# A third matmul level in one more round, stores moved to another queue, and a new table for side work

## The chip, the cores and the metric

The kernel runs on one core of a Trainium2 chip. The metric is the time of one execution on the device in microseconds (us); the median of several runs stands for a kernel. One execution was also profiled. Engines go by these names: PE (TensorE, matmuls), PEld (its weight loads), DVE (VectorE), ACT (ScalarE), POOL (GpSimd), and SP (SyncE, which here only issues DMAs). ACT and POOL issue DMAs too. Each engine works through its own queue in order.

## The reference

Two blocks, each with a residual, on x of shape (32, 128, 2048), in float32:

```python
x = x + L0_ffn(L0_cond(x, cond_128, ...), W, bias, A, Bf, coeffs, scales)
x = x + L1_ffn(L1_cond(x, cond_128, weight, c_weight, fside), up, down, perm)

# L0_cond: a mix of 8 kernels of 128x128 for each of 32 items
att = softmax(mlp(cond));  agg_w = einsum('bk,koi->boi', att, weight)
out = einsum('boi,bih->boh', agg_w, x) + (att @ bias_k)[:, :, None]
# L0_ffn: a dense 2048x2048 product with 16 low-rank updates
out = einsum('bsd,od->bso', x, W) + bias + updates(A, Bf, coeffs * scales)
# L1_cond: grouped convolution over the 2048 columns, 9 taps
# L1_ffn: a permutation of the columns, 16 heads of 128 -> 512 -> 128 with gelu, permuted back
```

The change concerns the dense product of L0_ffn (its weight, with the updates added in, is called W below) and the making of the mixed kernels agg_w.

## The kernel before

**The dense product.** It is done by a scheme that replaces eight products of half-size blocks by seven, nested. The outer seven are the *rounds* P1, P2, P6, P7, P5, P3, P4 in this order (`ROUNDS`). Each round goes over eight groups of four items, so a *step* is one round and one group, and the steps 0 to 7 of a round come one after the other. Inside a step the same seven-product scheme is used again (`multiply`): 28 matmuls of 512 columns. Two further functions take two neighbouring steps together, a *pair* (an even step, then an odd one):

- `multiply_third` (L579): the inner products P2 and P4 of both steps are not done one by one but by a third level, as seven *quarter* products (L603, matmuls of 256 columns at L611) that are all done in the odd step. The five other inner products stay (L598). A pair has 40 matmuls of 512 columns and 28 of 256.
- `multiply_more` (L484): the inner products P3 and P7 too are done at the third level. There are now two families of quarters (0 for P2 and P4, 1 for P3 and P7), three inner products (P1, P5, P6; matmuls at L501), and 24 matmuls of 512 columns and 56 of 256 (L516) in a pair. The even step does the quarters P1 and P2 of both families, the odd step the rest.

`PAIRS` says which pairs of a round have a third level, `MORE` which have it for P3 and P7 too: one pair of P6, three of P7, three of P3.

**Accumulators.** Each product sits in one of eight PSUM banks and is added by DVE to accumulators in SBUF (L497, L591), a quarter at L529 or L619. A quarter of family 1 needs a second addition of 256 columns (L534). Products that share a bank follow each other: quarters P1, P6, P7 and P4 of a family, and P5 and P3. Rounds P1 to P3 add to one accumulator, P5 to two (`ADDED`: u1 to u3 and u2 to c11). The accumulators come from DRAM (`part_load`) and go back (`part_store`) at the end of the odd step. P1 starts them: its first sums are copied by ACT (L593).

**Inputs and weights.** POOL makes the sums that the scheme needs: of x at L283 and L319 to L322 for a step ahead, of two steps at L444 (`third_inputs`) and L472 to L475 (`more_inputs`), of the weights at L252 to L256 (`inner_weights`), L401 to L407 (`third_weights`) and L462 (`more_weights`, whose second half DVE does at L1319). All of this lives in 26 equal SBUF buffers; a load waits for the last reader of the tile that had its buffer.

**W itself** is made in round P1: `w_make` for the first four blocks, `w_make_two` (L218) for twelve more, two ahead of each of steps 0 to 5, on PE (L223) and DVE (L226). The blocks are stored to DRAM (`w_store`, L168) through POOL's queue.

**Mixed kernels.** `mixed_kernel` (L708) makes an item's mixed 128x128 kernel by eight DVE operations (L716 the first, L718 the others). There are 256 of these. They are laid in between the products of a step, at the places `between(0)` to `between(3)` (a *turn* below): two at each in most steps of P2, P6, P7, P5 and P3, one in some, and 16 in all in the last two steps of P1. Each finished kernel is stored through ACT (L720).

Of the kernel before, what the change touches and what calls it, by code (L numbers as in the profile page):

```python
# [17 lines left out]
B = 32  # L18
L = 2048
QW = 512  # L20
KEXP = 8
# [11 lines left out]
NG = B // GB  # L33
# [18 lines left out]
    "P1": (0, 1, 2, 3), "P2": (0, 1, 2, 3), "P6": (0, 1, 2, 3), "P7": (0, 1, 2, 3),  # L52
    "P5": (0, 1, 2, 3), "P3": (0, 1, 2, 3), "P4": (0,),
}
MORE = {"P6": (1,), "P7": (1, 2, 3), "P3": (1, 2, 3)}
ENDS = ("P1", "P4")
EARLY = 2

# [2 lines left out]
def adaln_ffn_kernel(  # L61
# [16 lines left out]
    nc = tc.nc  # L78
# [85 lines left out]
        nc.sync.dma_start(t.rearrange("p k o c -> p (k o c)"), WT[kh, oh, kc])  # L164
        return t

    def w_store(k, t):
        nc.gpsimd.dma_start(wb_d[k], t.rearrange("p k o c -> p (k o c)"))  # L168

    def w_make(k, t, between=lambda: None):  # L170

# [46 lines left out]
    def w_make_two(ks, ts, sa, tb):  # L218
        pxs, pys, pzs = ([bank() for _ in ks] for _ in range(3))

        def product(n, ps, first, last, ki, oi):
            for (_, _, kc), p, t in zip(ks, ps, ts):
                nc.tensor.matmul(  # L223
                    p, lhsT=sa[n][:, kc], rhs=tb[n], start=first, stop=last, skip_group_check=True
                )
                nc.vector.tensor_tensor(t[:, ki, oi], p, t[:, ki, oi], ALU.add)  # L226

        product("P1", pxs, True, False, 0, 0)
        product("P2", pzs, True, True, 0, 0)
        done(*pzs)  # L230
        product("P6", pxs, False, False, 0, 1)
        product("P5", pys, True, False, 1, 1)
        product("P7", pxs, False, False, 1, 1)
        product("P3", pys, False, True, 0, 1)
        done(*pys)
        product("P4", pxs, False, True, 1, 0)
        done(*pxs)
        for k, t in zip(ks, ts):
            w_store(k, t)

    def row_sums(oh, t):
        for ki in range(2):
# [33 lines left out]
    def part_store(n, g, t, eng=nc.gpsimd):  # L276
        eng.dma_start(part_d[n, g], t.rearrange("p k s c -> p (k s c)"))
# [301 lines left out]
    def multiply_third(r, g, lhs, rhs, olds, between, quarters, sq):  # L579

        px, py = bank(), bank()
        accs = olds if olds[0] is not None else [slot(f"m_{r}{g}", (P, 2, 2, QW))]
        fresh = set()
        if sq:
            both = [held.pop(), accs]

        def add(si, oi, ps):
            for acc in accs:
                to = acc[:, si, oi]
                if olds[0] is not None or (si, oi) in fresh:  # L590
                    nc.vector.tensor_tensor(to, ps, to, ALU.add)  # L591
                else:
                    nc.scalar.copy(to, ps)  # L593
            fresh.add((si, oi))

        def product(k, ps, first, last):
            for kc in range(4):
                nc.tensor.matmul(  # L598
                    ps, lhsT=lhs[k][:, bass.ts(kc, P)], rhs=rhs[k][kc],
                    start=first and kc == 0, stop=last and kc == 3, skip_group_check=True,  # L600
                )

        def quarter(k, to):  # L603

            if k in ("P1", "P5", "P2"):
                qs[k] = bank()
            ps = qs[{"P6": "P1", "P7": "P1", "P4": "P1", "P3": "P5"}.get(k, k)]
            first, last = k in ("P1", "P2", "P5"), k in ("P2", "P3", "P4")
            for i, out in enumerate(halves(ps)):
                for kc in range(2):  # L610
                    nc.tensor.matmul(  # L611
                        out, lhsT=sq[k][:, i, bass.ts(kc, P)], rhs=quarters[i][k][kc],
                        start=first and i == 0 and kc == 0, stop=last and i == 1 and kc == 1,
                        skip_group_check=True,
                    )
            b, h = to
            for acc in both[b]:
                part = acc[:, :, 0, h * NQ : (h + 1) * NQ]
                nc.vector.tensor_tensor(  # L619
                    part, ps.rearrange("p (s n) -> p s n", s=2), part, ALU.add  # L620
                )
            if last:
                done(ps)

        qs = {}
        turns = [
            (("P1", (0, 0)), ("P2", (0, 0))), (("P6", (0, 1)), ("P5", (1, 1))),
            (("P7", (1, 1)), ("P3", (0, 1))), (("P4", (1, 0)),),
        ]

        def turn(n, now):
            if sq and now:
                for k, to in turns[n]:
                    quarter(k, to)

        early = r not in ENDS
        product("P1", px, True, False)
        add(0, 0, px)
        between(0)
        turn(0, early)  # L640
        if sq:
            sums_rest(nc.vector)
        product("P5", py, True, False)
        add(1, 1, py)
        between(1)
        turn(1, early)
        product("P6", px, False, False)
        add(0, 1, px)
        between(2)
        turn(2, early)  # L650
        product("P3", py, False, True)
        add(0, 1, py)
        done(py)
        between(3)
        turn(3, early)
        product("P7", px, False, True)
        add(1, 1, px)
        add(1, 0, px)
        done(px)
        turn(0, not early)  # L660
        between(4)
        turn(1, not early)
        turn(2, not early)
        between(5)
        turn(3, not early)
        if not sq:
            held.append(accs)
            return
        for b, accs in enumerate(both):
            for (_, new), acc in zip(ADDED[r], accs):  # L670
                part_store(new, g - 1 + b, acc, nc.sync)

    held = []

# [542 lines left out]
    olds = {}  # L1217
    chain = small()
    nxt, waiting, ts, quarter_ops, more_ops = {}, {}, {}, [], []
    heads = [(g, h) for g in range(NG) for h in range(NH)]  # L1220

    def olds_load(i):
# [3 lines left out]
    for i, (r, g) in enumerate(steps):  # L1226
        ri = i // NG
        last_round = ri + 1 == len(ROUNDS)
        if g == 0:
            b = (ri - 1) * (NG - 2) + 2  # L1230
            mixes = [(b + n // KEXP, n % KEXP) for n in range((NG - 2) * KEXP)]
            mixes = [m for m in mixes if m[0] < B]
        if i + 1 < len(steps):
            if i + 1 not in xs:
                xs[i + 1] = x_loads(*steps[i + 1])
# [62 lines left out]
        def between(j):  # L1298

            if j == 3 and 0 <= k_early < EARLY:  # L1300
                outer_sums(k_early, early_x)

            b = (ri - 1) * (NG - 2) + g + 1 if ri > 0 else g - (NG - 2)
            if (g in range(1, NG - 1) if ri > 0 else g >= NG - 2) and b < B and r not in MORE:
                k = j - 2 if r == "P5" and g == 1 else j
                if 0 <= k < KEXP // 2:
                    mixed_kernel(b, (2 * k, 2 * k + 1))
            if r in MORE and 0 < g and j < 4:
                for _ in range(1 if g in (2, 4) else 2):
                    if mixes:  # L1310
                        b, k = mixes.pop(0)
                        mixed_kernel(b, (k,))
            if ri == 0 and j == 2:
                for k in blocks[6 + 2 * g : 8 + 2 * g]:
                    wt[k] = w_load(*k)
            if i and j < 4 and quarter_ops:
                nc.vector.tensor_tensor(*quarter_ops.pop(0), ALU.subtract)
            if j < 4 and more_ops:
                nc.vector.tensor_tensor(*more_ops.pop(0), ALU.subtract)  # L1319
            if i == NG - 1 and j == 3:  # L1320
                olds_load(i + 1)
            if j == 3 and ahead and steps[i + 2][0] == "P6":
                xs[i + 2] = x_loads(*steps[i + 2])
            if ri == 0 and unsummed and (j in (1, 3) and (i, j) != (1, 3) or (i, j) == (3, 2)):
                row_sums(*unsummed.pop())
            if (i, j) in ((2, 5), (3, 0), (3, 4), (4, 0)) and unsummed_first:
                t = unsummed_first.pop(0)
                tt = nc.vector.tensor_tensor
                tt(wsum[:, 0, 0], wsum[:, 0, 0], t[:, 0, 0], ALU.add)
                tt(wsum[:, 0], wsum[:, 0], t[:, 1], ALU.add)  # L1330
            if last_round:
                if j == 1 and i + 1 < len(steps):
                    lhs[i + 1] = x_combine(*steps[i + 1], xs.pop(i + 1))
                    olds_load(i + 1)
                if j == 4 and i + 2 < len(steps):
                    xs[i + 2] = x_loads(*steps[i + 2])
                if j in (2, 4):
                    stage(k0 + j // 2, stage_first)
                if j % 2:
                    stage_third(k0 + j // 2)  # L1340
                else:
                    stage(k0 + j // 2, stage_second)
# [25 lines left out]
        if g == NG - 1 and ri + 1 < len(ROUNDS):  # L1368
            rhs = nxt
            nxt = {}  # L1370

    before = None
    for k, (g, h) in enumerate(heads):
# [83 lines left out]
```

## Time and profile before

| | |
|---|---|
| time, median of 3 runs | 2572.88 us (2571.82 to 2573.05) |
| the profiled execution | 2571.83 us, its span 2570.1 us |
| granted PE clock | 0.999 |
| PE busy | 2557.3 us |
| DVE busy | 1622.3 us |
| POOL busy | 1425.2 us |
| ACT busy | 532.4 us |
| round P5, pairs 0 to 3 (first product to first product) | 46.4 us each |
| round P3, pairs 1 to 3 | 45.0, 45.7, 45.1 us |

A window of the trace gives each engine's busy time in a pair. P5's pairs 1 to 3 are the windows from 895.1, 941.5 and 987.9 us, P3's those from 1080.8, 1125.8 and 1171.5. In them DVE is busy for 35.5, 35.6 and 26.7 us in P5 (the last has no mixed operations), and 33.6, 29.4 and 34.4 us in P3; POOL for 22.5, 25.4 and 25.9 us in P5, and 44.3, 37.6 and 38.9 us in P3. Lines of the page and of the trace name an engine, a line of the kernel, the operation, the tiles written and read, and shapes; what stands after an arrow is who ended the wait. In a timeline the first two numbers are the start and the length in us of operations that were merged (x2, x3).

### The profile page before, as it was taken

Reading aid. Unit: us, or ns where it says so; the run is one execution under the profiler, and the core shown is the slowest. Engines: PE = TensorE matmul, PEld = TensorE weight load, DVE = VectorE, ACT = ScalarE, POOL = GpSimd, SP = SyncE. Lnnn points to the kernel's source line nnn. Section 1 sums busy time; section 2 is a strip of 40 time slices with the busy share of each in tenths; the row PEclk is TensorE's granted clock in tenths of the full one; section 3 lists DMA queues with packets and bytes.
Section 4 is the critical chain, followed back from the end, with each engine's and each line's share of the span. In section 5 each row is a group of like instructions: output and inputs, shape, how many; then the busy total and the mean of one; then the engine's idle time right before and its main releaser. Section 6 shows DMA issues by size and latency. Waiting matters only on the chain.

```text
span 2570.1 us, 22392 instructions
## 1 busy us (share of the span) xinstructions
PE 2557.3 (100%) x7238; PEld 1373.2 (53%) x7238; DVE 1622.3 (63%) x2505; ACT 532.4 (21%) x1099; POOL 1425.2 (55%) x1182
## 2 busy tenths in 40 slices
PE   9999999999999999999999999999999999999998
PEld 4555555565566555566554454455554555555543
DVE  5575576676767777667477666666666666666610
ACT  0000000000000000000011344444434444444432
POOL 8532788889997846988532144444334434434222
PEclk9999999999999999999999999999999999999999
DMA  7552588569366586674866987777776787777432
GB/s 294 209 214 117 197 342 345 207 266 394 148 247 265 207 344 261 232 286 163 280 235 206 296 292 253 222 250 239 227 224 228 249 254 221 221 248 241 165 120 90
DMA packets 186868, 610.44 MB, mean 238 GB/s; under 512 B 17664, under 2 KB 91904, under 8 KB 142336
## 3 DMA queue, kind: packets, MB, share of 16 engines
q1 hardware_dynamic: 147936, 473.48, 51.4%
q0 software_dynamic: 32992, 132.14, 15.3%
q10 hardware_dynamic: 5824, 3.40, 0.5%
q8 instruction: 58, 0.95, 0.1%
q14 instruction: 58, 0.48, 0.1%
HBM read 372.45 MB, written 202.94 MB: 224 GB/s over the span
## 4 chain that ended last, share of the span: by engine, by line
PE 98%; DVE 2%; DMA 0%; issue 0%; POOLq 0%; ACT 0%; ACTq 0%; DVEq 0%
PE bank L598 24%; PE bank L990 17%; PE bank L1001 17%; PE bank L611 8%; PE bank L846 6%; PE bank L516 6%; PE bank L501 6%; PE bank L357 5%; PE bank L754 4%; PE bank L223 3%; PE bank L180 1%; DVE ags L718 1%; DMA w<-in_WT 0%; PE bank L157 0%; DVE u L497 0%; DVE u L529 0%
## 5 line engine op out<-in xcount | busy, mean ns | idle before, releaser
L990 PE MATMUL bank<-t,ws 128*128 128x512 f32 x1024 | 460.3, 592 | 0.0
L1001 PE MATMUL bank<-gl,ws 128*128 128x512 f32 x1024 | 460.2, 592 | 0.0
L1008 POOL DMA_INDIRECT out<-t,orow x128 | 153.1, 1196 | 547.6 <-DVE t L1006 471.6
L993 ACT ACTIVATE gl<-bank 128x512 f32<-128x512 f32 x512 | 306.2, 598 | 433.4 <-PE bank L990 424.0
L1001 PEld LDWEIGHTS bank<-gl,ws 128*128 128x128 f32 x1024 | 194.6, 190 | 233.0 <-issue 231.3
L990 PEld LDWEIGHTS bank<-t,ws 128*128 128x128 f32 x1024 | 194.6, 190 | 226.6 <-issue 223.1
L1006 DVE TENSOR_TENSOR t<-bank,t 128x512 f32<-128x512 f32 x128 | 88.5, 691 | 324.0 <-PE bank L1001 322.8
L739 POOL TENSOR_TENSOR x<-x,fb 128x512 f32<-128x512 f32 x128 | 174.7, 1393 | 178.3 <-DMA x<-in_x 139.2
L745 ACT ACTIVATE bank<-w,aggb 128x512 f32<-128x512 f32 x128 | 80.8, 684 | 876.7 <-DMA w<-w_d 864.2
L598 PE MATMUL bank<-P_t,s_P 128*128 128x512 f32 x576 | 255.6, 592 | 0.4 <-ACT m_P L593 0.4
L283 POOL TENSOR_TENSOR xt<-xt,xt 128x512 f32<-128x512 f32 x120 | 158.0, 1348 | 88.8 <-DMA xt<-in_xT 70.5
L718 DVE SCALAR_TENSOR_TENSOR ags<-mix,att_bc,ags 128x128 f32<-128x128 f32 x224 | 204.4, 913 | 4.3
L319 POOL TENSOR_TENSOR s_P<-xt 128x512 f32<-128x512 f32 x52 | 69.0, 1326 | 196.9 <-DMA xt<-in_xT 130.1
L598 PEld LDWEIGHTS bank<-P_t,s_P 128*128 128x128 f32 x576 | 109.4, 190 | 127.4 <-issue 123.5
L974 POOL DMA_INDIRECT t<-hx_d,row x128 | 131.4, 1027 | 53.3 <-issue 25.3
L591 DVE TENSOR_TENSOR u<-bank,u 128x512 f32<-128x512 f32 x132 | 85.4, 686 | 94.8 <-PE bank L598 91.7
L598 PE MATMUL bank<-wo_P,s_P 128*128 128x512 f32 x320 | 142.1, 592 | 0.0
L846 PE MATMUL bank<-va,tw_l 128*128 128x256 f32 x512 | 121.6, 380 | 0.8 <-DVE va L830 0.7
L857 ACT ACTIVATE cv<-bank,ctxb 128x128 f32<-128x128 f32 x256 | 73.0, 368 | 233.8 <-PE bank L846 233.8
L591 DVE TENSOR_TENSOR p<-bank,p 128x512 f32<-128x512 f32 x84 | 56.6, 688 | 102.2 <-PE bank L598 100.9
L846 PEld LDWEIGHTS bank<-va,tw_l 128*128 128x128 f32 x512 | 97.0, 190 | 42.4 <-issue 31.1
L757 DVE TENSOR_TENSOR x<-bank,x 128x512 f32<-128x512 f32 x128 | 88.2, 691 | 48.8 <-PE bank L754 19.7
(239 smaller groups left out, 4043.1 us busy)
## 6 DMA issues: line engine op xcount, KB each, us to landing
xt<-in_xT SPq DMA_DIRECT2D x84, 1024.0 KB
u<-u_d SPq DMA_DIRECT2D x40, 1024.0 KB
wo_P<-wb_d SPq DMA_DIRECT2D x36, 1024.0 KB
u<-c_d SPq DMA_DIRECT2D x64, 512.0 KB
x<-in_x SPq DMA_DIRECT2D x32, 1024.0 KB
xg<-x SPq DMA_DIRECT2D x256, 128.0 KB
hx_d<-x1t SPq DMA_DIRECT2D x32, 1024.0 KB
hx_d<-ht SPq DMA_DIRECT2D x32, 1024.0 KB
```

Source lines behind the costliest of these rows:

```text
L283: nc.gpsimd.tensor_tensor(out[:, i, j], a[:, i, j], b[:, i, j], op)
L501: nc.tensor.matmul(ps, lhsT=lhs[k][:, bass.ts(kc, P)], rhs=rhs[k][kc], start=first and kc == 0, stop=last and kc == 3, skip_group_check=True,)
L516: nc.tensor.matmul(out, lhsT=x[k][:, 1 - i if n else i, bass.ts(kc, P)], rhs=quarters[i][k][kc], start=first and i == 0 and kc == 0, stop= ...
L598: nc.tensor.matmul(ps, lhsT=lhs[k][:, bass.ts(kc, P)], rhs=rhs[k][kc], start=first and kc == 0, stop=last and kc == 3, skip_group_check=True,)
L611: nc.tensor.matmul(out, lhsT=sq[k][:, i, bass.ts(kc, P)], rhs=quarters[i][k][kc], start=first and i == 0 and kc == 0, stop=last and i == 1 ...
L718: nc.vector.scalar_tensor_tensor(ag, mix[:, k], att, ag, ALU.mult, ALU.add)
L739: nc.gpsimd.tensor_tensor(xt[:, f], xt[:, f], late["fb"][:, f], ALU.add)
L846: nc.tensor.matmul(out, lhsT=w[:, 2 * i + r], rhs=rhs, start=first and r == 0, stop=last and r == 1, skip_group_check=True,)
L990: nc.tensor.matmul(pu, lhsT=w[:, m * P : (m + 1) * P], rhs=t[:, 0], start=True, stop=True)
L993: nc.scalar.activation(gl[m], pu, AF.Gelu)
L1001: nc.tensor.matmul(pd, lhsT=w[:, (MC + m) * P : (MC + m + 1) * P], rhs=gl[m], start=(m == 0), stop=(m == MC - 1),)
L1008: nc.gpsimd.indirect_dma_start(out=out, out_offset=bass.IndirectOffsetOnAxis(ap=orow[:, g, h : h + 1], axis=0), in_=t[:, 1], in_offset=None,)
```

## The change

- `MORE` gets P5's pairs 1, 2 and 3.
- The twelve W blocks of `w_make_two` are stored through ACT's queue, not POOL's.
- The accumulators of round P1 are stored through ACT's queue, not SP's, after the same additions.
- The places of the mixed operations now stand in a table, `MIXES`: so many in each of the turns 0 to 3 of a step. Items and operations are taken from one list in order.

```diff
-MORE = {"P6": (1,), "P7": (1, 2, 3), "P3": (1, 2, 3)}
+MORE = {"P6": (1,), "P7": (1, 2, 3), "P3": (1, 2, 3), "P5": (1, 2, 3)}
+MIXES = {
+    "P1": (0, 0, 0, 0, 0, 0, 2, 5),
+    "P2": (0, 2, 2, 2, 2, 2, 2, 2),
+    "P6": (0, 2, 1, 2, 2, 2, 2, 2),
+    "P7": (0, 2, 1, 2, 1, 2, 2, 1),
+    "P5": (0, 1, 0, 1, 0, 1, 2, 2),
+    "P3": (0, 2, 1, 2, 1, 2, 2, 2),
+    "P4": (0,) * 8,
+}
...
-    def w_store(k, t):
-        nc.gpsimd.dma_start(wb_d[k], t.rearrange("p k o c -> p (k o c)"))
+    def w_store(k, t, eng=nc.gpsimd):
+        eng.dma_start(wb_d[k], t.rearrange("p k o c -> p (k o c)"))
...
         for k, t in zip(ks, ts):
-            w_store(k, t)
+            w_store(k, t, nc.scalar)
...
-                part_store(new, g - 1 + b, acc, nc.sync)
+                part_store(new, g - 1 + b, acc, nc.scalar if r == "P1" else nc.sync)
...
+    mixes = [(b, k) for b in range(B) for k in range(KEXP)]
...
-        if g == 0:
-            b = (ri - 1) * (NG - 2) + 2
-            mixes = [(b + n // KEXP, n % KEXP) for n in range((NG - 2) * KEXP)]
-            mixes = [m for m in mixes if m[0] < B]
...
-            if (g in range(1, NG - 1) if ri > 0 else g >= NG - 2) and b < B and r not in MORE:
-                k = j - 2 if r == "P5" and g == 1 else j
-                if 0 <= k < KEXP // 2:
-                    mixed_kernel(b, (2 * k, 2 * k + 1))
-            if r in MORE and 0 < g and j < 4:
-                for _ in range(1 if g in (2, 4) else 2):
+            if j < 4:
+                for _ in range(MIXES[r][g]):
                     if mixes:
                         b, k = mixes.pop(0)
                         mixed_kernel(b, (k,))
```

Before the change P5 had 48 of the 256 mixed operations, after it 28; P7 48 and 44, P6 48 and 52, P2 48 and 56, P1 16 and 28 (eight in step 6 both times, and 8 and 20 in step 7), P3 48 both times.

More of the change, by code (lines that the diff above doesn't have):

```diff
@@ L1370, in adaln_ffn_kernel @@
             nxt = {}
+    assert not mixes
     before = None
```

## The prediction

> **What bounds the kernel now.** I read the page's busy shares and its chain first, then the waits of PE, then single steps of the third-level rounds in the timelines of PE and DVE.
>
> ```profile
> PE 2557.3 (100%) x7238; PEld 1373.2 (53%) x7238; DVE 1622.3 (63%) x2505; ACT 532.4 (21%) x1099; POOL 1425.2 (55%) x1182
> PE 98%; DVE 2%; DMA 0%; issue 0%; POOLq 0%; ACT 0%; ACTq 0%; DVEq 0%
> PE bank L223 <- DVE w L226: 1.7, 1, 1.7
> PE bank L516 <- DVE u L534: 1.4, 2, 0.7
> ```
>
> PE is never idle: it stands still for 5.9 us in all its waits. So time falls only by less PE work, or by those few waits, and rises by every new wait of PE. The 1.7 us is at 137.8 us: a W load waited for its buffer (the chain of waits shows it landing after "133.80 4.87 DMA w<-in_WT"), because the store that empties that buffer stood at the end of POOL's queue until 125.15.
>
> The waits at L516 are in the pairs with a third level for P3 and P7, which is what the change adds to P5. Here are the last DVE and PE pieces of such an odd step (P3, step 5), DVE first:
>
> ```profile
> 1160.41 1.89 DVE L497 TENSOR_TENSOR u<-bank,u 128x512 f32<-128x512 f32 x3 [1.60 <-PE bank L501]
> 1162.21 2.52 DVE L718 SCALAR_TENSOR_TENSOR ags<-mix,att_bc,ags 128x128 f32<-128x128 f32 x2
> 1164.65 0.68 DVE L529 TENSOR_TENSOR u<-bank,u 128x512 f32<-128x512 f32 x1
> 1165.25 0.41 DVE L534 TENSOR_TENSOR u<-bank,u 128x256 f32<-128x256 f32 x1
> 1165.59 0.68 DVE L529 TENSOR_TENSOR u<-bank,u 128x512 f32<-128x512 f32 x1
> 1166.18 2.52 DVE L718 SCALAR_TENSOR_TENSOR ags<-mix,att_bc,ags 128x128 f32<-128x128 f32 x2
> 1168.63 0.68 DVE L529 TENSOR_TENSOR u<-bank,u 128x512 f32<-128x512 f32 x1
> 1169.23 0.41 DVE L534 TENSOR_TENSOR u<-bank,u 128x256 f32<-128x256 f32 x1
> ```
>
> ```profile
> 1167.11 1.89 PE L516 MATMUL bank<-wo_P,sv 128*128 128x256 f32 x8
> 1169.69 1.99 PE L516 MATMUL bank<-P_v,s_P 128*128 128x256 f32 x8 [0.69 <-DVE u L534]
> ```
>
> The reader sees a chain through one bank: the last quarter product (second family, P4) may write its bank only when DVE has read that family's P7 from it (1169.56), and DVE gets there through everything queued before: P6's adds, two mixed operations, two quarters, two mixed operations. Without the wait it starts at 1168.84. The starts give DVE's prices: an add of 512 columns out of PSUM 0.60 us, one of 256 columns 0.34, so a quarter of the first family 0.60 and of the second 0.94 for each accumulator.
>
> The mixed operations (L718) have two prices:
>
> ```profile
> 1001.86 1.29 DVE L591 TENSOR_TENSOR u<-bank,u 128x512 f32<-128x512 f32 x2 [1.50 <-PE bank L598]
> 1003.07 0.73 DVE L718 SCALAR_TENSOR_TENSOR ags<-mix,att_bc,ags 128x128 f32<-128x128 f32 x2
> ```
>
> Two of them took 0.73 us here, where POOL's timeline is empty, and 2.52 above, where it is full. Over all such pairs of operations with POOL at work the mean is 2.16 us (1.2 to 2.8); a single one costs 0.35 to 1.27 (mean 0.56). Adds out of PSUM cost the same either way.
>
> **Part 1, the third level in P5's pairs 1 to 3.** Each pair exchanges 16 matmuls of 512 columns for 28 of 256. A matmul leaves two records in this trace. In P5's pairs now, the chain has 56 records of 512 columns in 24.03 us, that is 0.858 us a matmul, and 16 of 256 columns in 3.45, that is 0.431. So a pair goes from 40 x 0.858 + 28 x 0.431 = 46.40 us (the trace: a first product at 891.66, 938.08, 984.50, 1030.92, so 46.42) to 24 x 0.858 + 56 x 0.431 = 44.74 (P3's three such pairs: 45.02, 45.73, 45.06, with their waits). Three pairs: -5.0 us of PE.
>
> What it puts on the others: P5 feeds two accumulators, where P7 and P3 feed one. A pair's 7 quarters of the second family cost 7 x 2 x 0.94 = 13.2 us of DVE on top of the 38 adds it has (26.7 us busy in the pair 987.9 to 1034.3), so 39.9 of 44.7. POOL gets four more input sums a pair (1.27 each, 5.1 us) and once eight weight differences of 0.75; DVE gets eight more in steps 1 and 2. These have room, except in the chain shown above. With two accumulators, P6's six adds are read from 17.40 us after the odd step's start (as in the trace, 1143.0 to 1160.4), and then follow 3.6, m, 1.87, 1.2, m, 1.87, where m is the mixed work between two products: the last reading ends at 25.9 + 2m. PE would start the P4 quarter at 25.84, and starts 0.13 after the reading. The wait is 0.2 + 2m: with one mixed operation a turn (steps 3 and 5) 0.9 us if POOL is idle, 2.8 at 1.27 each.
>
> **Step 3**: POOL is busy then (in the trace it works on inputs at 928.8 to 944, the end of the odd step); at a mean 0.5 the wait is 1.2. **Step 5**: POOL's inputs for step 7 cannot start there, see below, so 0.35 a piece: 0.9. **Step 1** keeps its form, but gets four weight differences: 0.2 for a quarter that comes as DVE is full (bounds 0 and 1).
>
> **Steps 6 and 7** have two mixed operations a turn. In the changed program the buffers that x for step 7 is loaded into are those that step 5's P4 quarter reads last. So these loads are issued some 24 us into step 5 and land 4.5 to 7 us later (a lone load takes 4.5, the next 2.45 more), 2.7 us into step 6, where in the trace POOL had that work from 974.88, 13 us before step 6. Eight operations for step 7, eight quarter inputs, eight for the next round and sixteen weight operations, 1.27 us each, then fill POOL through both steps, so mixed operations go at 2.1 a pair. DVE's queue in step 6 (us after its start): P1's adds end 4.8, mixed 6.9, P5's four adds 9.5, mixed 11.6, P6's six 15.2, mixed 17.3, two quarters 19.7, mixed 21.8, two quarters of the second family 25.5. PE is through at 17.2, so DVE carries 8.3 us into step 7. There (after step 7's start): P1's adds 9.6, mixed 11.7, quarters P6 and P5 12.9 and 14.1, P5's adds 16.5, mixed 18.6, P6 of the second family 20.4, P7 21.6, P6's adds 25.2, mixed 27.3, quarters 29.2 and 30.4, mixed 32.5, P7 34.4. PE against it: P7's quarter waits for the reading of P6's, 12.04 to 12.95; P3's of the second family for P5's, 25.0 to 29.3; P4's for P7's, to 34.5. Step 7 ends at 36.2 in place of 27.55: **+8.6 us**. Bounds: 0.73 a pair and no backlog, 0.2 + 2 x 0.7 = 1.6; 2.7 a pair, the highest row (2.79) less the overlap, 13.3. I take 8.6, as POOL's own list is longer than these steps.
>
> [...]
>
> Next behind a late step 7: the four accumulators' stores on SP, then the next loads. Those for P3 have a whole step (17 us) against 12 to 15 us of landing, so nothing is added. P3's inner weights wait for the last reading of P5's, which is now the first family's P3 quarter, 21.6 us into step 7. Their first part is ready 10.4 us later, before the product that needs it at 39.6.
>
> **Part 2, the first round's stores on ACT.** Twelve W stores leave POOL (0.55 us each, and 9.8 us of waiting for DVE) and eight partial stores leave SP, where they held the loads behind them. Twenty issues of 0.35 to 0.74 go to ACT, which has four copies a step there. Behind a store stand the next step's copies; the first is due 3.6 us into the step, the store waits for adds that end 1.3 us after the step before, and PE needs the copy only at 6.9: no cost (without that cover about 1.3 us in each of four pairs). The W store that went out at 125.15 goes out when its adds end (116.9), so the late load comes some 8 us earlier and the 1.72 us wait goes: -1.7 (bounds 0 and -2.1, with the 0.4 us that PE waits for ACT's copy at 255.8).
>
> **Part 3, mixed operations moved.** Of 256, P5 has 28 in place of 48, P7 44 in place of 48, P6 52 for 48, P2 56 for 48, P1 28 for 16, of which 20 in its last step, five a turn. P2 and P6 have one accumulator and two such pairs of products wait for nothing now: 0. In P1's last step these 20 stand ahead of the P7 add and the quarters. Now, POOL is at work there until 293.4, because x for that step came after the stores on SP (POOL waits "36.69 <-DMA xt<-in_xT" up to 257.53). With the stores gone that load needs only the second combination of B, last read at 219.3, and POOL is through at about 271.5 (its 14 last weight operations start when P1's P4 quarter ends, 248.5, then four input sums). DVE starts the twenty at 272.4, after the row sum's load (271.64 now), so 20 x 0.36 = 7.2 us lie within 10 us of products: 0. If POOL were as late as now, 15 of them at 1.27 would end at 291.4, the P7 add at 295.4, and the quarter P6 would start at 296.2 in place of 286.8: +9.3.
>
> **Sum.** -5.0 - 1.7 + 0.2 + 1.2 + 0.9 + 8.6 = +4.2 us. The profiled execution took 2571.83 (span 2570.1), so 2576.0; the median of the runs is 2572.88, 1.05 above it, so **2577.1 us**. A measurement of this kernel tells 0.2%, 5.1 us, from no change: the forecast is "no change that can be told", near its upper edge.
>
> **Rivals.**
> - *The mixed operations fall into POOL's gaps* (pairs of operations of 1.2 to 1.8 us occur at 917, 1056 and 1070 us; against it, POOL's 40 operations in steps 6 and 7). Steps 3, 5, 7 cost 0.9, 0.9, 1.6: -5.0 - 1.7 + 3.4 + 0.2 = -3.1, so 2569.8. Without any wait -6.7, 2566.2; only this is faster by over 0.2%, and 0.2 + 2m speaks against it.
> - *Slower: DVE becomes the bound of P5's last pair outright.* Place: steps 6 and 7; price: the mixed pairs at 2.7 and singles at 1.27, so 13.3 + 2.8 + 2.8 + 0.2 - 6.7 = +12.4, 2585. For it: rows of 2.73 at 977 and 1180; it decides from about 2.2 us a pair on, where the sum passes 5.1.
> - *POOL stays late in P1's last step*: +4.2 + 9.3, 2586. Against it: nothing but the queue of SP holds that load in the trace.
>
> **How the numbers follow.** The forecast's case 0.55 (its own range 2572 to 2580, the pair's mean between 1.7 and 2.4), gaps 0.2, DVE bound 0.17, late POOL 0.08. Above +5.1 lie 0.2 of the first case and both last ones: 0.45. Below -5.1 lies half of the gaps' case, 0.10. The rest is 0.45. For 8 in 10 the range goes from the gaps' value, 2569, to 2584.
>
> **What would show it.** PE's waits in the profile after: L525 (the quarters' new line) waiting for DVE u L543 in P5's steps 3, 5, 7, the last with over 6 us in three places; P5's pairs at about 46.0, 45.7 and 53.4 us in place of 46.4; no wait of L232 for DVE near 138; POOL idle from 272 to 283. The forecast is wrong if P5's last pair takes under 48 us or over 57, or if P1's last step waits.

## The result, and the profile after

| | before | after |
|---|---|---|
| median of 16 runs, us | 2572.31 (2570.09 to 2576.57) | 2577.97 (2574.79 to 2581.86) |
| profiled execution, us | 2571.83 | 2578.29 |
| its span, us | 2570.1 | 2576.5 |

The ratio is 1.0023, 95% interval 1.0016 to 1.0030. By it the change is 5.9 us slower (5.7 by the medians), on the bound of 0.2% that this kernel can tell from no change. The forecast was 2577.1.

The busy times on the page of the changed kernel:

```profile
PE 2556.5 (99%) x7310; PEld 1387.7 (54%) x7310; DVE 1653.5 (64%) x2597; ACT 532.4 (21%) x1099; POOL 1434.0 (56%) x1190
```

What PE waited for in it (us in total, times, longest):

```profile
PE bank L525 <- DVE u L543: 7.8, 5, 3.2
PE bank L620 <- DVE m_P L628: 1.0, 1, 1.0
PE bank L232 <- DVE w L235: 0.8, 1, 0.8
```

The first line is the quarters of the third level, all five times in P5 (the two waits of this kind before, 1.4 us, were in P7 and P3; they are not in this profile, but other profiles after the change have them again). The other two are new waits in P1; the 1.7 us of the weights' sums at 138 us is gone.

First products of pairs show where the 6.4 us of span lie (us, start of one pair to the next):

| | start of P5 | P5 pair 0 | pair 1 | pair 2 | pair 3 | P3 pair 0 | rest |
|---|---|---|---|---|---|---|---|
| before | 848.67 | 46.42 | 46.42 | 46.42 | 46.42 | 46.42 | |
| after | 849.20 | 46.42 | 47.21 | 45.62 | 51.21 | 47.51 | |
| change | +0.53 | 0 | +0.79 | -0.80 | +4.79 | +1.09 | 0 |

Two of these numbers are sums of larger ones. The +0.53 holds 1.1 us in the first 10 us, 0 from the waits near 138, 171 and 181 us together (below), +0.5 from there to P7, and -1.2 in P7, where the wait of 0.7 is absent. The 0 of the rest is -1.4 in P3's pairs 1 to 3, where the other such wait is absent, and +1.4 behind P3, a stretch that the change doesn't touch and that takes 1351.6 to 1355.6 us in the profiles at hand. Against this spread the differences in P5 are steady: nearly all of the loss is the end of P5's last pair. Its last three quarters on PE, from the timeline of the changed kernel (start, duration, and in brackets the idle time before):

```profile
1028.04 1.89 PE L525 MATMUL bank<-P_q,xt 128*128 128x256 f32 x8
1032.07 1.97 PE L525 MATMUL bank<-wo_P,sv 128*128 128x256 f32 x8 [2.13 <-DVE u L543]
1037.23 2.63 PE L525 MATMUL bank<-P_v,s_P 128*128 128x256 f32 x8 [3.20 <-DVE u L543]
1039.66 4.69 PE L607 MATMUL bank<-wo_P,xt 128*128 128x512 f32 x8
```

And the mixed operations (L725 the first of an item, L727 the others) of that step on DVE, with P6's six adds (L506):

```profile
1014.02 0.27 DVE L725 TENSOR_SCALAR ags<-mix,att_bc 128x128 f32<-128x128 f32 x1
1014.32 0.35 DVE L727 SCALAR_TENSOR_TENSOR ags<-mix,att_bc,ags 128x128 f32<-128x128 f32 x1
...
1019.38 1.66 DVE L727 SCALAR_TENSOR_TENSOR ags<-mix,att_bc,ags 128x128 f32<-128x128 f32 x2
...
1024.02 3.66 DVE L506 TENSOR_TENSOR u<-bank,u 128x512 f32<-128x512 f32 x6
1027.61 2.46 DVE L727 SCALAR_TENSOR_TENSOR ags<-mix,att_bc,ags 128x128 f32<-128x128 f32 x2
...
1033.04 2.28 DVE L727 SCALAR_TENSOR_TENSOR ags<-mix,att_bc,ags 128x128 f32<-128x128 f32 x2
```

The first two took 0.62 us, with POOL idle until 1014.59; each later pair 1.7 to 2.5. Between the two long ones DVE reads the banks that PE wants: PE stands still at 1029.94 to 1032.07 and at 1034.03 to 1037.23.

Look also at the durations on PE after the second wait: the same quarter takes 2.63 in place of 1.99, the next product 4.69 in place of 3.60 (the row of eight such matmuls elsewhere). The windows view of the changed kernel tells why; its columns are the stretch, its length, busy time of PE, PEld, DVE, ACT and POOL, the granted clock, the DMA share and GB/s:

```profile
1034.00:1036.00 2.00, 0.03 (x1) 0.00 (x0) 1.99 (x3) 0.00 (x0) 1.92 (x2) 1.00 0.00 0
1036.00:1038.00 2.00, 0.77 (x4) 0.69 (x5) 2.00 (x5) 0.00 (x0) 1.92 (x3) 1.00 0.11 33
1038.00:1040.00 2.00, 2.00 (x7) 1.66 (x6) 2.00 (x5) 0.00 (x0) 1.92 (x2) 0.61 0.00 0
1040.00:1042.00 2.00, 2.00 (x3) 0.67 (x2) 2.00 (x5) 0.00 (x0) 2.00 (x3) 0.54 0.96 393
1042.00:1044.00 2.00, 2.00 (x6) 0.95 (x5) 0.09 (x1) 0.00 (x0) 2.00 (x2) 1.00 1.05 434
```

The clock was at a half from 1038.4 to 1041.8, after the wait was over: 0.64 + 1.09 = 1.7 us more, of which 1.09 is the longer first pair of P3.

In P1 the stores' move gave and took. Before, DVE's row sum (first line) and ACT's table load for the exponential (second) were like this:

```profile
169.51 1.23 DVE L1330 TENSOR_TENSOR wsum<-wsum,w 128x1024 f32<-128x1024 f32 x1
166.06 1.28 ACT L1069 ACT_TABLE_LOAD   x1
178.16 0.21 ACT L1069 ACTIVATE small<-small 32x8 f32<-32x8 f32 x1 [10.82 <-DVE small L1068]
```

In the changed kernel:

```profile
168.62 2.31 DVE L1332 TENSOR_TENSOR wsum<-wsum,w 128x1024 f32<-128x1024 f32 x1
168.59 1.26 POOL L328 TENSOR_TENSOR s_P<-xt 128x512 f32<-128x512 f32 x1 [17.09 <-DMA xt<-in_xT]
176.19 2.05 ACTq L286 DMA_DIRECT2D p_d<-m_P  x2
178.27 1.28 ACT L1078 ACT_TABLE_LOAD   x1 [13.11 <-DVE small L1076]
```

An earlier x puts POOL's sums beside the row sum, which takes 1.1 us longer (PE waits 0.96 at 171.68). And the pair's store, issued by ACT at 176.19 once its additions were done, stands in front of the table load, which used to be over 12 us ahead of its use (PE waits 0.77 at 181.66). By the starts of PE's matmuls, PE loses 2.0 us at these two places and gains 2.0 at 138.

### The profile page after: what moved, and what is told of

It is laid out like the page before. It is cut to its first block, busy times and chain, and to the rows that moved or that the text cites. A ratio compares the mean times of both kernels' runs of the same rounds, so it can differ in the third digit from the quotient of the medians.

```text
span 2576.5 us, 22669 instructions
## 1 busy us (share of the span) xinstructions
PE 2556.5 (99%) x7310; PEld 1387.7 (54%) x7310; DVE 1653.5 (64%) x2597; ACT 532.4 (21%) x1099; POOL 1434.0 (56%) x1190
## 5 line engine op out<-in xcount | busy, mean ns | idle before, releaser
L607 PE MATMUL bank<-P_t,s_P 128*128 128x512 f32 x480 | 213.4, 592 | 0.5 <-ACT m_P L602 0.4
L727 DVE SCALAR_TENSOR_TENSOR ags<-mix,att_bc,ags 128x128 f32<-128x128 f32 x224 | 198.2, 885 | 4.2
L607 PEld LDWEIGHTS bank<-P_t,s_P 128*128 128x128 f32 x480 | 91.0, 190 | 107.7 <-issue 102.1
L510 PE MATMUL bank<-P_t,s_P 128*128 128x512 f32 x320 | 142.2, 592 | 0.0
L506 DVE TENSOR_TENSOR u<-bank,u 128x512 f32<-128x512 f32 x144 | 91.0, 683 | 79.7 <-PE bank L510 61.1
L538 DVE TENSOR_TENSOR u<-bank,u 128x512 f32<-128x512 f32 x168 | 111.2, 679 | 15.1 <-PE bank L525 14.4
```

What stands on the lines that cost most here:

```text
L510: nc.tensor.matmul(ps, lhsT=lhs[k][:, bass.ts(kc, P)], rhs=rhs[k][kc], start=first and kc == 0, stop=last and kc == 3, skip_group_check=True,)
L538: nc.vector.tensor_tensor(part, ps.rearrange("p (s n) -> p s n", s=2), part, ALU.add)
L607: nc.tensor.matmul(ps, lhsT=lhs[k][:, bass.ts(kc, P)], rhs=rhs[k][kc], start=first and kc == 0, stop=last and kc == 3, skip_group_check=True,)
L727: nc.vector.scalar_tensor_tensor(ag, mix[:, k], att, ag, ALU.mult, ALU.add)
```

## Experiments

Ratios are against the kernel before, run on the same chip. "Pairs" are P5's pairs 1, 2, 3 and P3's first pair, in us, each from the profile of that run.

| run | median, us | ratio | 95% interval | pairs |
|---|---|---|---|---|
| the change | 2577.97 | 1.0023 | 1.0016 to 1.0030 | 47.21, 45.62, 51.21, 47.51 |
| e1_p5_tail_clear | 2574.84 | 1.0005 | 0.9996 to 1.0014 | 46.16, 45.62, 45.09, 46.46 |
| e2_step7_clear | 2575.19 | 1.0011 | 1.0002 to 1.0020 | 46.15, 45.62, 45.09, 47.50 |
| e3_step6_clear | 2581.76 | 1.0035 | 1.0021 to 1.0049 | 46.17, 45.62, 51.85, 46.88 |
| e10_step7_first_turn | 2574.55 | 1.0007 | 0.9998 to 1.0016 | 46.16, 45.62, 45.09, 46.42 |
| e4_stores_back | 2589.26 | 1.0062 | 1.0048 to 1.0076 | 47.07, 45.62, 52.54, 47.62 |
| e5_stores_alone | 2571.34 | 1.0000 | 0.9991 to 1.0009 | 46.42, 46.42, 46.42, 46.42 |
| e6_third_level_alone | 2587.59 | 1.0056 | 1.0043 to 1.0070 | 48.92, 47.58, 52.92, 47.52 |
| e7_without_third_level | 2571.26 | 0.9995 | 0.9986 to 1.0004 | 46.42, 46.42, 46.42, 46.42 |
| e8_even_steps | 2570.27 | 0.9992 | 0.9983 to 1.0001 | 45.08, 45.09, 45.09, 48.00 |
| e9_blocks_on_pool | 2573.04 | 1.0000 | 0.9991 to 1.0009 | 45.09, 45.10, 45.09, 47.30 |
| e11_even_steps_p3_on_dve | 2571.47 | 0.9994 | 0.9985 to 1.0003 | 45.10, 45.09, 45.09, 47.81 |
| e12_best | 2569.27 | 0.9989 | 0.9980 to 0.9998 | 45.10, 45.09, 45.09, 47.83 |

### Is it the mixed operations, and those of which step?

Four runs move mixed operations out of P5's last two steps. First, all of them:

```diff
-    "P6": (0, 2, 1, 2, 2, 2, 2, 2),
+    "P6": (0, 2, 1, 2, 3, 3, 3, 3),
-    "P5": (0, 1, 0, 1, 0, 1, 2, 2),
+    "P5": (0, 1, 0, 1, 0, 1, 0, 0),
```

> P5's last two steps issue no mixed operation; their 16 go to P6's steps 4 to 7, three a turn there. Theory (the mixed operations of P5's steps 6 and 7, lengthened while POOL works, make VectorE late for the last pair's quarters, and the long wait then halves TensorE's clock): the last pair of P5 takes about 45.2 us instead of 51.21 (44.74 plus 0.2 and a restart), the granted clock stays at 1.00, P3's first pair falls from 47.51 to 46.4, the span by 7.1 us, the median to 2570.9. Rival 1 (the quarters' own additions into two accumulators are too much for VectorE, whatever is mixed): the last pair stays above 49 us, the median above 2576. Rival 2 (three a turn in P6 costs what is gained): P5's last pair falls as in the theory and P6's second half grows by 5 us or more; the median stays near 2577.

The pair fell to 45.09 and P3's first to 46.46, the clock stayed at 1.00: the theory's part of it, and rival 1 is out. But the median is 2574.84, 3.9 above the theory, since rival 2 holds in part (3.6 us in P6, under its 5). The waits of PE in this run:

```profile
PE bank L620 <- DVE p L628: 3.1, 2, 1.6
PE bank L525 <- DVE u L543: 2.2, 3, 1.1
```

Both waits of the first line are in P6, at 651.0 and 659.6, behind runs of three mixed operations of 3.3 us; they delayed PE by 3.6 us against before. All runs with three a turn in P6's last steps (e1, e2, e3, e10) carry 3.2 to 3.6 us of this.

Pair 1 takes 46.16 here, not 47.21, though its own operations are as in the changed kernel: one of step 3's two took 0.34 us, as it started 0.1 us ahead of an operation of POOL, where it took 1.45 in the changed kernel. The prediction's rule gives 0.2 + 0.34 + 0.89 = 1.43 over 44.74, and 1.42 was measured.

Then one step at a time. Step 7 cleared, and below it step 6:

```diff
-    "P6": (0, 2, 1, 2, 2, 2, 2, 2),
+    "P6": (0, 2, 1, 2, 2, 2, 3, 3),
-    "P5": (0, 1, 0, 1, 0, 1, 2, 2),
+    "P5": (0, 1, 0, 1, 0, 1, 2, 0),
```

> Only P5's step 7 is without mixed operations, step 6 keeps its eight. Own-work theory (the wait of step 7's last quarters is the mixed operations issued in that step, two runs of 2.3 to 2.5 us right ahead of them): waits of 0.4 us or less in step 7, P5's last pair 45.2 us, clock 1.00, median 2570.9. Carry theory (the lateness that step 6 hands on is enough): the carry of 3.5 us seen at step 7's first addition is worked off in 24 us only in part, and a wait of 1 to 3 us stays before the last quarter; last pair 46 to 48 us, median 2572 to 2574.

```diff
-    "P6": (0, 2, 1, 2, 2, 2, 2, 2),
+    "P6": (0, 2, 1, 2, 2, 2, 3, 3),
-    "P5": (0, 1, 0, 1, 0, 1, 2, 2),
+    "P5": (0, 1, 0, 1, 0, 1, 0, 2),
```

> Only P5's step 6 is without mixed operations, step 7 keeps its eight. Own-work theory: by 0.2 + 2m with m = 2.37, the mean of the last two runs of step 7, the waits of step 7 stay at about 4.9 us; last pair about 50 us, and the clock is halved again if one wait is near 3 us; median 2575 to 2578. Carry theory: the 5.4 us of step 6's mixed runs that VectorE had no idle time for are gone from its backlog, waits in step 7 fall to about 0.4 us, last pair 45.3 us, median 2571.

With step 7 empty the last pair takes 45.09, the same as with both steps empty: step 6's eight operations cost it nothing. With step 6 empty it takes 51.85, no less than in the changed kernel. PE and DVE in e3, step 7:

```profile
1034.66 1.97 PE L525 MATMUL bank<-wo_P,sv 128*128 128x256 f32 x8 [2.14 <-DVE u L543]
1039.84 3.27 PE L525 MATMUL bank<-P_v,s_P 128*128 128x256 f32 x8 [3.21 <-DVE u L543]
1018.77 2.49 DVE L506 TENSOR_TENSOR u<-bank,u 128x512 f32<-128x512 f32 x4 [2.14 <-PE bank L510]
1021.17 2.45 DVE L727 SCALAR_TENSOR_TENSOR ags<-mix,att_bc,ags 128x128 f32<-128x128 f32 x2
1026.61 3.66 DVE L506 TENSOR_TENSOR u<-bank,u 128x512 f32<-128x512 f32 x6
```

DVE is idle for 2.14 us before 1018.77, half way through the step, so nothing of step 6 is left over there, and still PE's waits are 2.14 and 3.21, as in the changed kernel (2.13 and 3.20). The carry theory falls; the own-work theory holds. Both medians lie above what was expected: e2's by P6's 3.4 us and by a wait of 0.80 for POOL in P3's first pair, which is new; e3's by P6 and the halved clock.

Is it their number, or POOL beside them and their place? The same as e3, but with all eight at the place where POOL has nothing to do:

```diff
-                for _ in range(MIXES[r][g]):
+                n = MIXES[r][g]
+                if (r, g) == ("P5", 7):
+                    n = 4 * n if j == 0 else 0
+                for _ in range(n):
```

> As the version with step 6 of P5 empty and eight mixed operations in step 7 (2581.8, waits of 2.1 and 3.2 us), but all eight stand in step 7's first turn, where POOL waits for its input (idle 4.8 us from about 1012.4 to 1017.2 in that version) and VectorE is on time. Theory (an operation is dear because POOL works beside it, 0.31 to 0.35 us without and 1.1 to 1.2 with): eight take 2.5 to 3.5 us, the last quarters wait less than 0.5 us in all, the clock stays at 1.00; median 2574 to 2575.5. Rival (eight operations in an odd step are too many wherever they stand): waits of 4 us or more in step 7, median 2579 to 2582.

The mixed operations of step 7, P6's adds and POOL's idle time in this run:

```profile
1013.75 0.28 DVE L725 TENSOR_SCALAR ags<-mix,att_bc 128x128 f32<-128x128 f32 x1
1014.06 2.67 DVE L727 SCALAR_TENSOR_TENSOR ags<-mix,att_bc,ags 128x128 f32<-128x128 f32 x7
1017.34 4.96 POOL L292 TENSOR_TENSOR xt<-xt,s 128x512 f32<-128x512 f32 x4 [3.97 <-DMA s<-s_d]
1026.32 3.68 DVE L506 TENSOR_TENSOR u<-bank,u 128x512 f32<-128x512 f32 x6 [1.35 <-PE bank L510]
```

Eight in 2.98 us, 0.37 each, all done before POOL starts again at 1017.34. No wait in step 7, the pair 45.09, the clock 1.00. The same eight operations cost 6.8 us in e3 (51.85 - 45.09), and nothing here, so it is not their number. Two things changed at once, the place and POOL's work beside them. The trace parts them by an estimate: behind the eight, DVE is idle for only 0.30 and 1.35 us before P6's adds, and not at all from there to the last reading. At 1.2 us each, as beside POOL in e3 (2.45 for two), the eight would have taken 6.6 us more, and some 5 of them would have come out as PE's wait. So the early place alone would not have made them free; no run puts eight there beside a busy POOL.

### What each part does alone

Part 2 alone, on the kernel before:

> The kernel before with the first round's stores on ScalarE's queue and nothing else. Theory (the recorded step: the stores' move takes away P1's late load of weights, -1.7 us): no wait of L232's counterpart for VectorE near 138 us, nothing in its place; median 2570.6. Rival (what the changed kernel's trace suggests: the wait goes, -2.0, but x for step 5 of P1 lands earlier, so that POOL's input sums lengthen VectorE's row sum near 168 us, and the load of ScalarE's table for the exponential comes 12 us later, right ahead of its use near 178): two new waits of about 1.0 and 0.8 us, +2.0 together; median within 0.5 us of 2572.5.

```diff
-            w_store(k, t)
+            w_store(k, t, nc.scalar)
...
-                part_store(new, g - 1 + b, acc, nc.sync)
+                part_store(new, g - 1 + b, acc, nc.scalar if r == "P1" else nc.sync)
```

The waits are the rival's; the time, 1.0000 with 0.9991 to 1.0009, would allow either. What PE waits for in P1:

```profile
PE bank L223 <- DVE w L226: 1.2, 2, 0.8
PE bank L611 <- DVE m_P L619: 1.0, 1, 1.0
```

The 1.7 us near 138 is gone (the 0.45 in the first line is at 38 us, where P1 starts up), and 0.96 at 171 and 0.77 at 181 came. By the starts of its matmuls PE gains 2.0 us on the profile of before at the first place and loses 1.1 and 0.9 at the other two.

Part 1 alone, so that P5's odd steps keep two mixed operations a turn:

```diff
-MORE = {"P6": (1,), "P7": (1, 2, 3), "P3": (1, 2, 3)}
+MORE = {"P6": (1,), "P7": (1, 2, 3), "P3": (1, 2, 3), "P5": (1, 2, 3)}
```

> The kernel before with the third level in P5's pairs 1 to 3 and nothing else, so that P5's odd steps 3, 5 and 7 each issue two mixed operations a turn. Own-work theory (0.2 + 2m in an odd step, m = 1.6 to 2.4 a run while POOL works, as seen in step 7 of the changed kernel): waits of 3.4 to 5 us in each of three steps, 0.3 us more for each wait's restart, the clock halved after the longest; P5 +5 to +12 us against before, median 2578 to 2585. Rival (the added operations find VectorE idle): waits under 1 us in each, median 2568 to 2570.

1.0056, 14.4 us; the median is in neither's range but just above the theory's. Waits of 3.6, 2.3 and 4.8 us in the three steps (step 5's is smaller than expected), with the clock halved from about 1041.4 on (rows on PE of 3.06, 3.78 and 4.70 us in place of 1.97, 1.99 and 3.60), and 1.2 us in step 1, where DVE has eight mixed operations and four weight differences.

The changed kernel without part 1 (`MORE` as before):

> The changed kernel without the third level in P5: parts two and three alone. Theory (stores and moved operations cost nothing by themselves): no wait of the quarters in P5, P5's pairs at 46.4 us each, P1's last step without a wait, median 2571 to 2573. Rival (the operations moved to P7's, P2's or P1's steps are paid there): median over 2575, with waits in those rounds.

The theory holds: 0.9995, pairs at 46.42, no wait in P1's last step. A wait of 1.29 at 181 is there and the one near 138 is not. So, as differences of such ratios, the third level cost 14.4 us net with the old places, 5.9 + 1.3 = 7.2 us with the new ones.

The changed kernel without part 2 (the two stores as in the kernel before):

> The first round's stores go back to POOL's and SP's queues, all else as in the changed kernel. Theory (the third part of the change needs the second: with the stores on SP ahead of it, x for P1's last step lands near 257 us, POOL works until about 293, and the twenty mixed operations of that step take over 1 us each): TensorE waits in P1's last step for 5 to 9 us, the median is 2583 to 2587. Rival (the stores' queue matters nothing): no wait in P1's last step, median within 2 us of 2578.

The theory holds, and its upper end was passed: 2589.26. The timeline of P1's last step in this run, a line of POOL, one of DVE and two of PE:

```profile
256.92 1.26 POOL L328 TENSOR_TENSOR s_P<-xt 128x512 f32<-128x512 f32 x1 [36.82 <-DMA xt<-in_xT]
272.31 9.30 DVE L727 SCALAR_TENSOR_TENSOR ags<-mix,att_bc,ags 128x128 f32<-128x128 f32 x7
282.66 6.58 PE L607 MATMUL bank<-w,s_P 128*128 128x512 f32 x8 [3.30 <-ACT m_P L602]
295.59 6.97 PE L620 MATMUL bank<-P_q,sq 128*128 128x256 f32 x24 [2.90 <-DVE m_P L628]
```

Seven mixed operations in a row took 9.30 us, 1.33 each: about one POOL operation (1.27) for each of them, where in the changed kernel, POOL being idle from 273.0 to 284.8, seven take 2.68. PE loses 11.1 us in this step against before: 6.2 in the two waits, 4.6 by the halved clock (granted 0.50; 8 matmuls in 6.58 us in place of 3.60, 24 short ones in 6.97 in place of 5.34). The waits near 171 and 180 us are not there, so against the changed kernel some 9 remain. There is no wait near 138 either, with the stores as before the change: the load that came late there went out at 133.12 (before: 133.80). In e6 and e12, which also keep the first two pairs' stores where they were, the wait is there, 1.73 and 1.89. So it stands on an edge, and its absence in one profile is not the store's move alone.

### Versions that keep the gain

P5's 28 operations in steps that end none of the three changed pairs:

```diff
-    "P5": (0, 1, 0, 1, 0, 1, 2, 2),
+    "P5": (0, 1, 2, 0, 2, 0, 2, 0),
```

> The changed kernel with P5's 28 mixed operations all in steps that end no pair of the third level: four in step 1, eight each in steps 2, 4 and 6, none in 3, 5 and 7; the other rounds as they are. Own-work theory: all three pairs take 44.8 us, no quarter waits over 0.3 us, the clock stays at 1.00; the span is 2576.5 less 10.9 (the pairs' and P3's excess), 2565.6, the median 2567.1, faster than before by 0.2%. Carry theory: eight operations in an even step make the quarters of the odd step after it wait, 1 to 2 us in each of three; median 2570 to 2573.

All three pairs at 45.09: the own-work theory again. The median is 3.2 above it. Of that 1.0 is that 45.09, not 44.76, is what a pair takes without mixed operations; 1.6 is a new wait, the first of these two:

```profile
PE bank L620 <- POOL P_q L411: 1.3, 1, 1.3
PE bank L232 <- DVE w L235: 1.3, 1, 1.3
```

It is in P3's first pair, which takes 48.00: POOL got its input for P3's first step only at 1012.6 (5.15 us idle on a load) and from there worked without a pause to P3's quarter weights. In the changed kernel PE came to them only after step 7's waits, and didn't wait for them. The second line is the late table of P1, as in the changed kernel.

The same version with six of P3's eight weight differences on DVE (its expectation calls the late input that of P5's step 7; it is the one for P3's first step):

```diff
-                    tt(t[:, 0, kc], r12, r11, ALU.subtract)
-                    tt(t[:, 1, kc], r22, t[:, 0, kc], ALU.subtract)
+                    if name != "P3":
+                        tt(t[:, 0, kc], r12, r11, ALU.subtract)
+                        tt(t[:, 1, kc], r22, t[:, 0, kc], ALU.subtract)
+                    else:
+                        firsts += [(t[:, 0, kc], r12, r11), (t[:, 1, kc], r22, t[:, 0, kc])]
+                        lasts.append((t[:, 3, kc], r21, t[:, 1, kc]))
```

> The version with P5's mixed operations in even steps (2570.3), with six of the eight third-level weight operations of P3 on VectorE in P3's first step instead of POOL, since TensorE waited there 1.3 us for POOL (P3's first pair 1.8 us longer). Theory (the end of P5's waits made POOL, late because its input for P5's step 7 comes late, the next to be waited for): that wait goes, P3's first pair takes 46.4 us again, median 2568.5. Rival (POOL's inputs are late all the same, or VectorE becomes late in P3's first step): a wait of 0.5 us or more stays in P3's first pair, for POOL or VectorE; median 2569.5 to 2572.

The rival: P3's first pair takes 47.81, PE now waits for DVE there, 0.42 and 0.47. Nothing gained.

The blocks' stores back on POOL, the sums' stores left on ACT:

```diff
-            w_store(k, t, nc.scalar)
+            w_store(k, t)
-    "P5": (0, 1, 0, 1, 0, 1, 2, 2),
+    "P5": (0, 2, 2, 0, 2, 0, 1, 0),
```

> As the version with P5's mixed operations in even steps, but the weights' blocks are stored by POOL again (the sums of P1's pairs stay on ScalarE), and P5's numbers by step are 0, 2, 2, 0, 2, 0, 1, 0. If the blocks' stores on ScalarE are what brings P1's two new waits (table of the exponential loaded late; x of step 5 early, so POOL's sums beside VectorE's row sum): no wait near 171 and 180 us, and the wait near 138 us, 0.4 to 1.7, is back; sum over P1 within 0.5 us of before. If the sums' stores bring them, they stay. Step 6 with half its mixed operations should shorten POOL's wait chain little: P3's first pair still waits for POOL, 1.0 to 1.3 us. Median 2569.5 to 2571.

The wait for the late table stays, 1.27 us at 180.8, so the sums' stores bring it. The one near 138 is not back, with the load issued at 123.83: to move the sums' stores is enough for that. The wait near 171 isn't there, nor is it in e7 and e8, where the blocks are on ACT. It goes with who starts first: in the seven profiles with this wait (the changed kernel, e1, e2, e3, e5, e10, e11) POOL's first sum starts 0.02 to 0.16 us ahead of the row sum, which then takes 2.2 to 2.3; in e7, e8 and e9 it starts 0.04 to 0.65 behind, takes 1.7 to 2.3 itself, and the row sum takes 1.23. The second operation a turn in step 1 of P5 cost 1.7 us (pair 0 takes 48.08). 2573.04, a miss.

From these, one more: step 7's operations in its first turn, step 6 empty, and only the sums of P1's last two pairs on ACT, which is after the exponential.

```diff
-            w_store(k, t, nc.scalar)
+            w_store(k, t)
-                part_store(new, g - 1 + b, acc, nc.scalar if r == "P1" else nc.sync)
+                part_store(new, g - 1 + b, acc, nc.scalar if r == "P1" and g >= 5 else nc.sync)
-    "P5": (0, 1, 0, 1, 0, 1, 2, 2),
+    "P5": (0, 1, 2, 0, 2, 0, 0, 2),
```

> The changed kernel with P5's mixed operations by step 0, 1, 2, 0, 2, 0, 0, 2, those of step 7 all in its first turn, and with only the last two pairs' sums of P1 stored by ScalarE (the blocks go back to POOL, the first two pairs' sums to SP). From the runs: the three pairs of P5 at 44.8 us without a wait of the quarters and P3's first pair at 46.4 (a step 6 without mixed operations left POOL in time there); the table of the exponential is loaded ahead of its use, so no waits near 171 and 180 us; the wait near 138 us is back with 0.4 to 1.7; x for P1's last step is in time, so no wait in it. Against the version with even steps (2570.3 beside a kernel before of 2571.8): -1.8 for P3, -1.5 to 0 for P1; median 2567.5 to 2569, ratio 0.998 to 0.999. Rival (each wait removed only uncovers the next): POOL is waited for in P3's first pair or P1's last step waits for the late x; median 2570 to 2573.

2569.27, 0.9989 with an interval of 0.9980 to 0.9998: faster than the kernel before by 2.8 us and the only one of all these whose interval lies under 1, though within the 0.2% of before. The pairs are as expected, the waits at 171 and 180 are gone, the one at 138 is back with 1.89. P3's first pair is not: 47.83, with 1.14 us for POOL, as the rival said. (e9 and this run differ in P1 in the stores of the first two pairs' sums: those bring the late table, and with them on ACT the wait near 138 is not there.) An empty step 6 alone doesn't bring POOL in time; in e10, where there is no such wait, the even steps before it were empty too.

## Why the prediction was nearly right

- **Products, -5.0 for three pairs**: right. With no mixed operation a pair takes 45.09, which is 44.74 and 0.35; the rule has 0.2 of this as a wait. (The starts that the prediction lists, 891.66 and on, are of a pair's last product, 3.43 before the next pair's first; their distance is the same.)
- **Step 1, +0.2**: 0; pair 0 still takes 46.42.
- **Steps 3 and 5, +1.2 and +0.9**: 47.21 and 45.62 less 44.74 are +2.47 and +0.88. The rule 0.2 + 2m gives these with the durations of the mixed operations in the trace: 1.45 and 0.83 in step 3 (m = 1.14), 0.34 in step 5. Only m of step 3 was mis-sized, at 0.5.
- **Step 7, +8.6**: 51.21 less 44.74 is 6.5, and 1.1 more falls on P3's first pair: 7.6. The size is near, and the x that lands late and fills POOL came as told (POOL got it at 989.83, 1.4 us into step 6). But the step "DVE carries 8.3 us into step 7" is wrong as a cause. DVE did end step 6 late (1012.82, 7.2 us after PE), but e3 has no carry and the same waits. What decides is the step's own runs, 2.46 and 2.28 us: 0.2 + 2 x 2.37 = 4.9. The halved clock, 1.7 us, which no step of the forecast had, brings it to 6.7; 0.9 remain. The rule lets P6's six adds begin 17.40 us after the step's start, as they do in e10 (17.41), but they begin 18.37 after it here and 18.36 in e3. In e3, without a carry, that is the run of 2.45 before them, for which the rule has no term. Here that run takes 1.66 and begins 0.8 later, so of the carry of 7.2 some 0.8 is left there. PE waited in two places, not three.
- **These terms together**: forecast +10.9 on top of the products; measured 0 + 2.47 + 0.88 + 7.56 = +10.9. That the sum agrees so closely is luck in its parts.
- **P1, -1.7**: the step that failed. The late load was issued at 123.55 in place of 133.80 and its wait went, as told. But "behind a store stand the next step's copies ... no cost" left out that the table load and the exponential stand there too, and the prediction doesn't ask what the x that comes earlier collides with. These two waits took the 2.0 us back, in e5 as in the changed kernel. Nor did the blocks' store have to leave POOL: in e9 it goes out there at 117.09 (before: 125.15), since x comes earlier and POOL is through sooner. P1 and what follows up to P5 came out at +0.5; 1.1 of it are in the first 10 us, in which other profiles lie up to 2.9 us behind that of before, and 1.2 less in P7 is the absent wait, so this number too is partly chance. This is the 2.2 us between the forecast's +4.2 and the span's +6.4.
- **Stores and P1's last step, 0**: right. POOL is idle from 273.0 to 284.8 (forecast: 272 to 283), the twenty operations cost nothing, and without the stores' move that step cost 11.1 (the rival's price was 9.3, without the halved clock).
- **Rivals**: gaps in POOL happened once in step 7 (0.62 for two), too little to help. The mean of the eight runs in steps 6 and 7 is 1.75 us, under the 2.1 assumed and the 2.2 from which DVE was to be the outright bound.

## What to carry to other kernels

Where two engines slow each other, as DVE and POOL do here (a mixed operation took 0.37 us with POOL idle in e10, 1.2 beside it in e3), an operation has no one price: find the stretch in which the other engine waits for its input and put the work there, away from the last readings; in this kernel the same eight operations cost 6.8 us or nothing within one step. When a store moves to another queue, list everything that stands behind it there, table loads too (here one came 12.2 us later and PE waited 0.77), and ask what the transfers that come earlier will run beside (here POOL's sums beside a row sum, 2.31 us in place of 1.23). A wait that is removed shows the next one: here POOL, late for P3's first input, took back 1.6 us.

## What the runs showed that was not expected

**A wait can halve the clock after it.** In the changed kernel waits of 2.13 and 3.20 us, with a quarter between them, were followed by 3.41 us at a granted clock of 0.50 (from 1038.44 to 1041.85). In e4, one of 2.32 us was enough, and as another of 2.30 fell into the slow stretch, it lasted from 1042.8 to 1053.1:

```profile
1040.00:1042.00 2.00, 0.07 (x1) 0.10 (x1) 2.00 (x5) 0.00 (x0) 1.92 (x2) 1.00 0.00 0
1042.00:1044.00 2.00, 2.00 (x7) 1.70 (x8) 1.97 (x4) 0.00 (x0) 1.92 (x3) 0.71 0.00 0
1044.00:1046.00 2.00, 0.80 (x2) 0.08 (x1) 2.00 (x3) 0.00 (x0) 1.92 (x2) 0.50 0.00 0
...
1050.00:1052.00 2.00, 2.00 (x5) 1.17 (x4) 1.18 (x4) 0.00 (x0) 2.00 (x3) 0.50 1.07 438
1052.00:1054.00 2.00, 2.00 (x4) 0.72 (x3) 0.87 (x2) 0.00 (x0) 2.00 (x3) 0.73 1.00 414
```

Yet in e6 waits of 0.61 and 3.03 us in step 3 left it at 1.00:

```profile
943.00:946.00 3.00, 1.11 (x6) 0.63 (x4) 2.96 (x5) 0.00 (x0) 2.92 (x3) 1.00 0.00 0
946.00:949.00 3.00, 1.87 (x9) 1.66 (x10) 3.00 (x7) 0.00 (x0) 3.00 (x4) 1.00 0.00 0
```

So the length of the wait alone doesn't tell. The clock records of the traces do. In e4 the clock falls at 281.67, 295.32 and 1042.84 us, whole multiples of 3.413 us apart, and each slow stretch in these runs, but for the start and the end of the program, is one, two or three times 3.41 long. Let the whole run be cut into stretches of 3.413 us that fit these falls, and PE's idle time be counted in each. In the one just before a fall it is 2.20 us (the changed kernel), 2.85 (e3), 2.31, 2.63 and 2.32 (e4) and 2.70 (e6). The most in a stretch that no fall follows, from 30 us on, is 1.75; the wait of 3.03 in e6 lies across two stretches, with 1.75 and 1.27. At half speed, a stretch with 0.85 to 1.45 us idle was followed by another slow one, and one with 0 to 0.27 by full speed. In these runs, then, a fall went with 2.20 us of idle time or more within one such stretch, and PE was still busy for 0.6 to 1.2 us in each stretch before a fall.

**A wait costs more than the view lists.** In the undisturbed pairs 1 and 2 of the changed kernel, 1.93 us in two waits and 0.57 in one came with 2.47 and 0.88 us over 44.74: some 0.3 us each. The rows show most of it: eight short matmuls are listed with 1.89 us though the next start 1.73 after them, so the first 0.16 of a wait is not listed as idle, and the eight after a wait take some 0.1 more (1.97 and 1.99).
